# Bilinear sampling weights as clamped ramps on row differences, half of the broadcast ones made on GpSimd

## The chip, the cores and the metric

The kernel runs on one core of a Trainium2 chip. The core has a matrix engine (TensorE, PE in the profile), a vector engine (VectorE, DVE), an engine for pointwise functions (ScalarE, ACT), a general engine (GpSimd, POOL) and a queue engine (SyncE, SP), and 16 DMA engines that serve all queues. The metric is the device time of one execution in microseconds. The kernel before takes 16,853.93 us, the median of three runs from 16,836.08 to 16,859.17.

## The reference

The network has four residual layers on an image batch of 16 x 32 x 128 x 128, in float32. Only layer 1 is touched, and of it the last part. That part samples each image at nine deformed positions per pixel, combines them with a 9-tap convolution and normalises:

```
y      = weight * yk + y_new                     # 9 row positions per pixel
ys     = clip(y_map, 0, H - 1)                   # fractional row
xs     = clip(x_map, 0, W - 1)                   # whole column: c + k - 4
deformed = grid_sample_bilinear(input, (xs, ys)) # two rows, weights 1-|y-p|
out    = conv2d(deformed, dsc_w, dsc_b, stride=(9, 1))
out    = group_norm(out, gn_w, gn_b, 8 groups);   x = x + out
```

The column is always a whole number, so a sample is a mix of two neighbouring rows of one column: row `p` has the weight max(0, 1 - |y - p|).

## The kernel before

The program runs its stages one after the other: layer 0, three stages of layer 1 (offset convolution, scan, sampling), layer 2, and two stages of layer 3. The sampling stage is `layer1_sample`, lines 1031 to 1312.

The interpolation is written as a matrix product over the rows. An image lies in SBUF as `xt`, 128 rows on the partitions, 32 channels times 128 columns along each. For one tap and one image column, the stationary operand is `xt[:, :, xc]` (128 rows x 32 channels) and the moving operand is a 128 x 128 tile that holds, for each of 128 positions `y` (free dimension), the weight of each image row `p` (partition). Four such products stand side by side in the matrix engine (function `sample`, line 1133).

The weights are made as hats. `|y - p|` needs `y` on all partitions. It gets there in two ways: the taps 0 to 3 by a product with a selecting matrix into PSUM (`spread`, matmul in line 1121), read by ScalarE with `Abs` and the bias `nrow` = -p (line 1122) into the tile `ya`; the taps 4 to 7 by a DMA that reads four rows of the position map and writes them to all 128 partitions (`fetch`, line 1111, 1 MB), the tile `yd`, on which ScalarE runs `Abs` in place (`absolutes`, line 1242). VectorE then turns both into min(|y - p|, 1) - 1, the hat with its sign turned (`hats`, line 1126). The ninth tap is made like `ya`, once per four blocks (`eighth`, tile `h8`, `last_tap`). The turned sign is undone in the convolution weights `w4` and `w8` (lines 1103 and 1105).

A block `m` is four image columns; an image has 32 blocks, the 16 images 512. The loop over `m` issues, in this order: on block 12 the loads of the next image (`open_image`, with `xt` in four quarters of eight channels, line 1099); the fetch for block m+3; the products of taps 0 to 3; `Abs` of `yd` and the hat of `ya` for block m+1; the copy of the products out of PSUM (line 1280); the spread for block m+2; the products of taps 4 to 7; the hat of `yd` for block m+1; the second copy (line 1286). Every four blocks follow the convolution (lines 1168 and 1173), a turn to rows on the partitions (line 1185), and the ninth tap. When an image is complete, `finish` normalises it in 22 small steps, one per block, and adds the input `xt` (line 1233); the result is stored by a DMA on GpSimd's queue (line 1234).

`in_order` (line 48) fixes the order of TensorE's, VectorE's and ScalarE's instructions to that of the program. SP, which issues the loads, is ordered by the planner. `yd` has four buffers, so a fetch waits until the products of the block four earlier have read its buffer; `xt` has two, and because `finish` adds the input, a buffer is held until the image after it is about two thirds done.

Of the kernel before, what the change touches and what calls it, by code (L numbers as in the profile page):

```python
# [10 lines left out]
F32 = mybir.dt.float32  # L11
AF = mybir.ActivationFunctionType
ALU = mybir.AluOpType
# [1017 lines left out]
def layer1_sample(tc, w, x1, x2, ymap, sb1, batches=range(B)):  # L1031
# [6 lines left out]


    nc = tc.nc  # L1040
    V, S, M = nc.vector, nc.scalar, nc.tensor.matmul
    W4 = 4 * HW
    NB = HW // 4
    batches = list(batches)
    with ExitStack() as ctx:
# [9 lines left out]
        nrow = load(nc, cp, w["nrow"], "nrow")  # L1055
        avg = cp.tile([P, P], F32, name="avg", tag="avg")
        V.memset(avg, 1.0 / P)

# [28 lines left out]
        def open_image(b):  # L1087
            im = images[b] = {}
            g, j = divmod(b, 4)
            im["Y"] = Y = yp.tile([P, W4], F32, name="Y", tag="Y")  # L1090
            nc.sync.dma_start(Y, ym(b)[0:4].rearrange("k (n f) -> (k n) f", f=W4))
            im["Y8"] = Y8 = yp.tile([P, W4], F32, name="Y8", tag="Y8")
            y8 = ym(b)[8].rearrange("(s q f) -> q s f", q=4, f=W4)
            for q in range(4):
                nc.sync.dma_start(Y8[32 * q : 32 * q + 8], y8[q])
            im["xt"] = xt = xp.tile([P, T, HW], F32, name="xt", tag="xt")
            xg = x1[g][T * j : T * j + T].rearrange("o (r c) -> r o c", c=HW)
            for q in range(4):
                nc.sync.dma_start(xt[:, 8 * q : 8 * q + 8], xg[:, 8 * q : 8 * q + 8])

            s = cb[:, g, j, 0:1]
            im["w4"] = w4 = sp.tile([P, 2, T], F32, name="w4", tag="w4")
            V.tensor_scalar(w4, dw4[:, :, 0:T], s, -1.0, ALU.mult, ALU.mult)
            im["w8"] = w8 = sp.tile([P, P], F32, name="w8", tag="w8")
            V.tensor_scalar(w8, dw8, s, -1.0, ALU.mult, ALU.mult)

        def fetch(m):
            b, n = order[m]
            blocks[m] = bl = {}
            bl["yd"] = yd = hp.tile([P, 4, W4], F32, name="yd", tag="yd", bufs=4)  # L1110
            nc.sync.dma_start(
                yd, ym(b)[4:8, n * W4 : n * W4 + W4].unsqueeze(0).to_broadcast([P, 4, W4])
            )

        def spread(dst, Y, n, k):

            for h in range(2):
                pb = psb.tile([P, 2, W4], F32, name="pb", tag="pb")
                for a in range(2):
                    q = 32 * (2 * h + a)  # L1120
                    M(pb[:, a], sel[q : q + k, n], Y[q : q + k], start=True, stop=True)  # L1121
                S.activation(dst[:, 2 * h : 2 * h + 2], pb, AF.Abs, bias=nrow)  # L1122

        def hats(t):

            V.tensor_scalar(t, t, 1.0, 1.0, ALU.min, ALU.subtract)  # L1126

        def sample(pd, b, todo):

# [5 lines left out]
                    start=True, stop=True, tile_position=(0, 32 * q),  # L1135
                )

        def taps(m, k0, h):
            b, n = order[m]
            pd = psd.tile([P, 4, HW], F32, name="pd", tag="pd")  # L1140
            sample(
                pd, b,
                [
                    (q, i, 4 * n + i + k0 + q - 4, h[:, q, HW * i : HW * i + HW])
                    for i in range(4) for q in range(4)
                ],
            )
            return pd
# [42 lines left out]
        def finish(b):  # L1191

            g, j = divmod(b, 4)
            im = images[b]
            ob, xt = im["ob"], im["xt"]
# [24 lines left out]
            V.tensor_mul(bi, sc, mean.unsqueeze(2).to_broadcast([P, 8, 4]))  # L1220
            V.tensor_sub(bi, rows[:, 1].rearrange("p (a b) -> p a b", b=4), bi)
            yield
            for q in range(4):
                o = slice(8 * q, 8 * q + 8)
                col = [
                    t.rearrange("p a b -> p (a b)")[:, o].unsqueeze(2).to_broadcast([P, 8, HW])
                    for t in (sc, bi)
                ]
                V.tensor_mul(ob[:, o], ob[:, o], col[0])
                yield  # L1230
                V.tensor_add(ob[:, o], ob[:, o], col[1])
# [8 lines left out]
        def absolutes(m):  # L1240
            yd = blocks[m]["yd"]
            S.activation(yd, yd, AF.Abs, bias=nrow)  # L1242

        def near(m):
            b, n = order[m]
# [6 lines left out]
            images[b]["h8", s] = h8  # L1252

        open_image(batches[0])
        NM = len(order)
        for m in range(min(3, NM)):
            fetch(m)
        with in_order(tc, nc.tensor, nc.vector, nc.scalar):
            eighth(batches[0], 0)
            near(0)  # L1260
            absolutes(0)
            near(1)
            hats(images[batches[0]]["h8", 0])
            hats(blocks[0]["ya"])
            hats(blocks[0]["yd"])
            done = iter(())
            for m in range(NM + 6):
                b, n = order[m] if m < NM else (None, m - NM)
                if m < NM:
                    bl = blocks[m]  # L1270
                    bl["ds"] = dp.tile([P, 2, W4], F32, name="ds", tag="ds", bufs=6)
                    if n == 12 and m + NB < NM:
                        open_image(order[m + NB][0])
                    if m + 3 < NM:
                        fetch(m + 3)
                    pd = taps(m, 0, bl["ya"])
                    if m + 1 < NM:
                        absolutes(m + 1)
                        hats(blocks[m + 1]["ya"])
                    V.tensor_copy(bl["ds"][:, 0], pd.rearrange("p i r -> p (i r)"))  # L1280
                    if m + 2 < NM:
                        near(m + 2)
                    pd = taps(m, 4, bl["yd"])
                    if m + 1 < NM:
                        hats(blocks[m + 1]["yd"])
                    V.tensor_copy(bl["ds"][:, 1], pd.rearrange("p i r -> p (i r)"))  # L1286
                s, i = divmod(n, 4)
                if i == 0 and 4 <= m <= NM:
# [6 lines left out]
                elif i == 1 and 5 <= m <= NM + 1:  # L1295
                    turn(bb, ss, oc)
                    if ss == NB // 4 - 1:
                        for _ in done:
                            pass
                        done = finish(bb)  # L1300
                elif i == 2 and m + 2 < NM:
                    nb_, nn = order[m + 2]
                    eighth(nb_, nn // 4)
                elif i == 3 and m < NM:
                    pd = last_tap(b, s, images[b].pop(("h8", s)))
                    ds8 = dp.tile([P, W4], F32, name="ds8", tag="ds8")
                    S.copy(ds8, pd.rearrange("p i r -> p (i r)"))
                    images[b]["ds8"] = ds8
                    if m + 1 < NM:
                        nb_, nn = order[m + 1]  # L1310
                        hats(images[nb_]["h8", nn // 4])
                next(done, None)
            for _ in done:
                pass
# [982 lines left out]
def pack(inp):  # L2297
# [105 lines left out]
    w["nrow"] = -np.arange(P, dtype=f)[:, None]  # L2403

    def conv(a):
        return _diag(a.reshape(a.shape[0], a.shape[1], 9).transpose(1, 2, 0), 4)
# [97 lines left out]
```

## Time and profile before

| | value |
|---|---|
| span of the profiled execution | 16,843.7 us |
| median of the runs | 16,853.93 us |
| PE, DVE, ACT, POOL busy in the whole span | 14,662.1, 14,631.9, 12,582.5, 9,561.6 us |
| sampling stage, 10,855 to 14,030 us: PE, ACT, DVE, POOL busy | 2,890.6, 2,794.6, 2,739.7, 93.2 us |
| granted TensorE clock and DMA share in the stage | 0.90, 0.78 |
| `ya` (L1122), two per block | 1,024 elements, mean 1,251 ns |
| `yd` (L1242), one per block | 2,048 elements, mean 2,421 ns |
| hats of `ya` and `yd` (L1126) | 2,048 elements, mean 1,478 and 1,414 ns |
| ScalarE's wait for the DMA of `yd` in the stage | 47.5 us in 13 waits |

The profiled execution's own time is its span, 16,843.7 us; the runs' median is 10 us longer, as it takes in what lies around the first and last instruction. Busy times overlap between engines. A group's mean duration is that of single instructions, which may overlap at their ends with the next.

### The profile page before, as it was taken

What the parts mean: (1) busy time and instruction counts of PE and PEld (TensorE: products, weight loads), DVE (VectorE), ACT (ScalarE), POOL (GpSimd) and SP (SyncE); (2) the same over time, 40 slices, a digit from 0 to 9 for tenths busy, and PEclk for the clock granted to TensorE, in tenths of its full rate; (3) what the DMA queues carried; (4) which work ended last, traced back from release to release, by engine and by line L of the source; (5) the groups of instructions that cost most, each with busy time, mean ns of one, the idle gap of its engine ahead of it and who ended that gap; (6) DMA issues with size and microseconds to landing.
All of it is one profiled execution on the core that took longest, in us unless ns stands there. A gap on an engine that the chain in (4) does not pass through costs nothing. (4 is left out here: it accounts for less than half of the span.)

```text
span 16843.7 us, 301825 instructions
## 1 busy us (share of the span) xinstructions
PE 14662.1 (87%) x113386; PEld 5677.8 (34%) x113386; DVE 14631.9 (87%) x14520; ACT 12582.5 (75%) x25308; POOL 9561.6 (57%) x17517
## 2 busy tenths in 40 slices
PE   8999999989999888988888888899999997688966
PEld 3333333333333222222222222255555553234421
DVE  9999999999999669999999999888888887788622
ACT  8999999999999557777777677688898883466411
POOL 8999999999999238778887788500000000000012
PEclk9999999999999989899999999899999898788977
DMA  0000000000000854445454445578877789644456
GB/s 22 13 12 13 13 17 13 13 12 13 18 13 8 136 139 164 154 161 163 168 166 163 156 161 168 159 187 197 200 199 194 193 192 195 129 79 83 79 147 201
DMA packets 1553471, 1898.99 MB, mean 113 GB/s; under 512 B 158053, under 2 KB 879710, under 8 KB 1543239
## 3 DMA queue, kind: packets, MB, share of 16 engines
q1 hardware_dynamic: 1440582, 1701.94, 38.7%
q0 software_dynamic: 31552, 127.40, 2.1%
q10 hardware_dynamic: 79872, 50.36, 1.2%
q8 instruction: 892, 14.61, 0.4%
q14 instruction: 573, 4.69, 0.1%
HBM read 1560.92 MB, written 229.64 MB: 106 GB/s over the span
## 5 line engine op out<-in xcount | busy, mean ns | idle before, releaser
L235 POOL TENSOR_SCALAR Rp<-su,nv 128x128 f32<-128x128 f32 x15360 | 5406.1, 371 | 167.7 <-PE pS L241 132.9
L239 ACT ACTIVATE Ra<-su,bv 128x128 f32<-128x128 f32 x15360 | 4625.8, 389 | 405.9 <-PE pS L241 402.6
L224 DVE TENSOR_TENSOR Rd<-pu,nv 128x2048 f32<-128x2048 f32 x2176 | 4856.6, 2275 | 19.6 <-PE pS L241 18.6
L241 PE MATMUL pS<-Rd,zw 128*32 128x512 f32 x17408 | 2794.8, 606 | 380.1 <-DVE Rd L224 379.4
L828 DVE TENSOR_TENSOR_SCAN hh<-dd,state,pd 128x512 f32<-128x512 f32 x2304 | 2823.3, 1267 | 152.6 <-PE py L862 9.6
L849 POOL TENSOR_TENSOR hh<-hh,bc 128x2048 f32<-128x2048 f32 x512 | 2319.0, 4530 | 451.2 <-DVE state L836 437.9
L1234 POOL DMA_DIRECT2D x<-ob x64 | 92.4, 1443 | 3106.4 <-DVE ob L1233 2769.9
L813 PE MATMUL pd<-du,spread 32*128 32x512 f32 x4608 | 1348.8, 659 | 553.3 <-DVE hh L828 545.7
L805 ACT ACTIVATE dd<-dd,m_a 128x512 f32<-128x512 f32 x2304 | 1513.1, 713 | 328.5 <-DMA dd<-dm 322.4
L823 DVE TENSOR_TENSOR pd<-pd,bc 128x1024 f32<-128x1024 f32 x1152 | 1401.0, 1216 | 53.4 <-ACT bc L786 51.4
L241 PE MATMUL pS<-Rp,zw 128*32 128x512 f32 x7680 | 1310.7, 597 | 25.3 <-POOL Rp L235 25.2
L1242 ACT ACTIVATE yd<-yd,nrow 128x2048 f32<-128x2048 f32 x512 | 1239.7, 2421 | 47.6 <-DMA yd<-ymap 47.5
L1122 ACT ACTIVATE ya<-pb,nrow 128x1024 f32<-128x1024 f32 x1024 | 1188.4, 1251 | 86.5 <-PE pb L1121 85.4
L241 PE MATMUL pS<-Ra,zw 128*32 128x512 f32 x7680 | 1235.7, 600 | 0.0
L1121 PE MATMUL pb<-Y,sel 32*128 32x512 f32 (+1 forms) x5120 | 1083.6, 742 | 167.5 <-ACT ya L1122 164.2
L241 PEld LDWEIGHTS pS<-Rd,zw 128*32 128x32 f32 x17408 | 580.8, 109 | 1487.5 <-DVE Rd L224 928.7
L813 PEld LDWEIGHTS pd<-du,spread 32*128 32x128 f32 x4608 | 372.8, 190 | 1594.7 <-DVE hh L828 714.4
L1126 DVE TENSOR_SCALAR yd<-yd 128x2048 f32<-128x2048 f32 x512 | 724.2, 1414 | 191.8 <-ACT yd L1242 190.9
L1126 DVE TENSOR_SCALAR ya<-ya 128x2048 f32<-128x2048 f32 x512 | 756.7, 1478 | 9.2 <-ACT ya L1122 7.6
L1133 PE MATMUL pd<-ya,xt 128*32 128x128 f32 x16384 | 690.7, 311 | 42.7 <-DVE ds L1286 31.3
L1133 PEld LDWEIGHTS pd<-yd,xt 128*32 128x32 f32 x16384 | 539.2, 178 | 469.9 <-issue 231.5
L1839 PE MATMUL ps<-t,W 128*128 128x512 f32 x1280 | 627.8, 637 | 64.2 <-DVE W L1819 56.5
(426 smaller groups left out, 23147.3 us busy)
## 6 DMA issues: line engine op xcount, KB each, us to landing
dd<-dm SPq DMA_DIRECT2D x2304, 256.0 KB
yd<-ymap SPq DMA_DIRECT2D x512, 1024.0 KB
hw<-x SPq DMA_DIRECT2D x192, 512.0 KB
dm<-dt POOLq DMA_DIRECT2D x192, 256.0 KB, 3.6
w<-d SPq DMA_DIRECT2D x512, 73.1 KB
xb<-tok SPq DMA_DIRECT2D x248, 144.0 KB
x<-in_x SPq DMA_DIRECT2D x64, 512.0 KB
x<-o SPq DMA_DIRECT2D x128, 256.0 KB
```

The source lines that it names most:

```text
L224: nc.vector.tensor_tensor(R, st["pu"].unsqueeze(1).to_broadcast([P, 4, 4, HW]), nv[:, :, i::32].rearrange("p t q -> p q t").unsqueeze(3).t ...
L235: nc.gpsimd.tensor_scalar(R[:, q, k], su[:, k], 3.4028234e38, nv[:, k, c], ALU.min, ALU.max)
L239: nc.scalar.activation(R[:, q, k], su[:, k], AF.Relu, bias=bv[:, k, c])
L241: nc.tensor.matmul(st["pS"][32 * q : 32 * q + 32], zw[:, 31 - i : 63 - i], R[:, q], start=first, stop=False, tile_position=(0, 32 * q), sk ...
L805: S.activation(dd[:, r], dd[:, r], AF.Exp, scale=acol[:, dr, d : d + 1])
L813: nc.tensor.matmul(pd[:, a], spread[e, k], st["du"][n][e], start=True, stop=True)
L823: V.tensor_mul(pd, pd, bm.unsqueeze(1).to_broadcast([P, 2, CH]))
L828: V.tensor_tensor_scan(hh[:, r, s], dd[:, r, s], pd[:, a, s], st["state"][:, 4 * i + r : 4 * i + r + 1], ALU.mult, ALU.add,)
L849: G.tensor_mul(hh, hh, st["bc"][1, n].unsqueeze(1).to_broadcast([P, 4, CH]))
L1126: V.tensor_scalar(t, t, 1.0, 1.0, ALU.min, ALU.subtract)
L1133: M(pd[32 * q : 32 * q + 32, i], xt[:, :, xc], h, start=True, stop=True, tile_position=(0, 32 * q),)
L1242: S.activation(yd, yd, AF.Abs, bias=nrow)
```

## The change

The sum over hats is rewritten by parts. With x[p] the rows of the image and y between 0 and 127, the sample is x[0] + sum over p of clamp(y - p, 0, 1) * (x[p+1] - x[p]). The moving operand thus holds ramps, max(y - p, 0) limited to 1, and the stationary operand holds differences of neighbouring rows. The last partition carries row 0: its bias is +1, so that its ramp is always 1.

- The `xt` tile is loaded from rows 1 to 127 and, on its last partition, row 0: two DMAs per quarter in place of one, of 127 rows and of one row.
- The plain rows are loaded as well, in quarters (`quarter`, tile `xq`, two buffers, on SP), and GpSimd subtracts them from `xt` on 127 partitions (`differ`), at the blocks 24 to 27 before the image is used; for the first image before the loop.
- `finish` adds `xq` quarters, loaded again, and no longer reads `xt`.
- `Abs` becomes `Relu` on ScalarE; VectorE's operation becomes a minimum with 1 (`clamps`), still in place.
- The fetch of taps 4 to 7 becomes two fetches of two rows each, `yd` (taps 4 and 5) and `ye` (6 and 7), 512 KB each, both with four buffers. ScalarE and VectorE treat `yd` as before at half the size. GpSimd makes the ramps of `ye` in two operations (`far`): add the bias and maximum with 0, then minimum with 1, two blocks ahead.
- GpSimd's instructions join the fixed order.

```diff
@@ open_image
             for q in range(4):
-                nc.sync.dma_start(xt[:, 8 * q : 8 * q + 8], xg[:, 8 * q : 8 * q + 8])
+                o = slice(8 * q, 8 * q + 8)
+                nc.sync.dma_start(xt[0 : P - 1, o], xg[1:P, o])
+                nc.sync.dma_start(xt[P - 1 : P, o], xg[0:1, o])
-            V.tensor_scalar(w4, dw4[:, :, 0:T], s, -1.0, ALU.mult, ALU.mult)
+            V.tensor_scalar_mul(w4, dw4[:, :, 0:T], s)
...
+        def quarter(b, q):
+            g, j = divmod(b, 4)
+            xq = xp.tile([P, 8, HW], F32, name="xq", tag="xq")
+            xg = x1[g][T * j + 8 * q : T * j + 8 * q + 8].rearrange("o (r c) -> r o c", c=HW)
+            nc.sync.dma_start(xq, xg)
+            return xq
+
+        def differ(b, q):
+            xt = images[b]["xt"][0 : P - 1, 8 * q : 8 * q + 8]
+            G.tensor_sub(xt, xt, quarter(b, q)[0 : P - 1])
@@ fetch
-            bl["yd"] = yd = hp.tile([P, 4, W4], F32, name="yd", tag="yd", bufs=4)
-            nc.sync.dma_start(
-                yd, ym(b)[4:8, n * W4 : n * W4 + W4].unsqueeze(0).to_broadcast([P, 4, W4])
-            )
+            for key, k in (("yd", 4), ("ye", 6)):
+                bl[key] = t = hp.tile([P, 2, W4], F32, name=key, tag=key, bufs=4)
+                nc.sync.dma_start(
+                    t,
+                    ym(b)[k : k + 2, n * W4 : n * W4 + W4].unsqueeze(0).to_broadcast([P, 2, W4]),
+                )
+
+        def far(m):
+            ye = blocks[m]["ye"]
+            G.tensor_scalar(ye, ye, step, 0.0, ALU.add, ALU.max)
+            G.tensor_scalar_min(ye, ye, 1.0)
@@ spread, hats
-                S.activation(dst[:, 2 * h : 2 * h + 2], pb, AF.Abs, bias=nrow)
+                S.activation(dst[:, 2 * h : 2 * h + 2], pb, AF.Relu, bias=step)
-            V.tensor_scalar(t, t, 1.0, 1.0, ALU.min, ALU.subtract)
+            V.tensor_scalar_min(t, t, 1.0)
@@ finish
+                xq = quarter(b, q)
...
-                V.tensor_add(ob[:, o], ob[:, o], xt[:, o])
+                V.tensor_add(ob[:, o], ob[:, o], xq)
@@ loop
-        with in_order(tc, nc.tensor, nc.vector, nc.scalar):
+        with in_order(tc, nc.tensor, nc.vector, nc.scalar, nc.gpsimd):
...
+                    if 24 <= n < 28 and m + NB < NM:
+                        differ(order[m + NB][0], n - 24)
                     if m + 3 < NM:
                         fetch(m + 3)
+                    if m + 2 < NM:
+                        far(m + 2)
...
-                    pd = taps(m, 4, bl["yd"])
+                    pd = taps(m, 4, bl["yd"], bl["ye"])
```

More of the change, by code (lines that the diff above doesn't have):

```diff
@@ L1040, in layer1_sample @@
     nc = tc.nc
-    V, S, M = nc.vector, nc.scalar, nc.tensor.matmul
+    V, G, S, M = nc.vector, nc.gpsimd, nc.scalar, nc.tensor.matmul
     W4 = 4 * HW
@@ L1054, in layer1_sample @@
         ident = load(nc, cp, w["ident"], "ident")
-        nrow = load(nc, cp, w["nrow"], "nrow")
+        step = load(nc, cp, w["step"], "step")
         avg = cp.tile([P, P], F32, name="avg", tag="avg")
@@ L1098, in open_image @@
             for q in range(4):
-                nc.sync.dma_start(xt[:, 8 * q : 8 * q + 8], xg[:, 8 * q : 8 * q + 8])
+                o = slice(8 * q, 8 * q + 8)
+                nc.sync.dma_start(xt[0 : P - 1, o], xg[1:P, o])
+                nc.sync.dma_start(xt[P - 1 : P, o], xg[0:1, o])
             s = cb[:, g, j, 0:1]
             im["w4"] = w4 = sp.tile([P, 2, T], F32, name="w4", tag="w4")
-            V.tensor_scalar(w4, dw4[:, :, 0:T], s, -1.0, ALU.mult, ALU.mult)
+            V.tensor_scalar_mul(w4, dw4[:, :, 0:T], s)
             im["w8"] = w8 = sp.tile([P, P], F32, name="w8", tag="w8")
-            V.tensor_scalar(w8, dw8, s, -1.0, ALU.mult, ALU.mult)
+            V.tensor_scalar_mul(w8, dw8, s)
+        def quarter(b, q):
[7 more added lines that the diff above has]
+            G.tensor_sub(xt, xt, quarter(b, q)[0 : P - 1])
         def fetch(m):
@@ L1121, in spread, with clamps @@
                     M(pb[:, a], sel[q : q + k, n], Y[q : q + k], start=True, stop=True)
-                S.activation(dst[:, 2 * h : 2 * h + 2], pb, AF.Abs, bias=nrow)
-        def hats(t):
-            V.tensor_scalar(t, t, 1.0, 1.0, ALU.min, ALU.subtract)
+                S.activation(dst[:, 2 * h : 2 * h + 2], pb, AF.Relu, bias=step)
+        def clamps(t):
+            V.tensor_scalar_min(t, t, 1.0)
         def sample(pd, b, todo):
@@ L1136, in sample, with taps @@
                 )
-        def taps(m, k0, h):
+        def taps(m, k0, *hs):
             b, n = order[m]
+            w = 4 // len(hs)
             pd = psd.tile([P, 4, HW], F32, name="pd", tag="pd")
@@ L1143, in taps @@
                 [
-                    (q, i, 4 * n + i + k0 + q - 4, h[:, q, HW * i : HW * i + HW])
+                    (q, i, 4 * n + i + k0 + q - 4, hs[q // w][:, q % w, HW * i : HW * i + HW])
                     for i in range(4) for q in range(4)
@@ L1194, in finish @@
             im = images[b]
-            ob, xt = im["ob"], im["xt"]
+            ob = im["ob"]
             st = sp.tile([P, 8, 6], F32, name="st", tag="st")
@@ L1238, in finish, with ramps @@
                 yield
-        def absolutes(m):
+        def ramps(m):
             yd = blocks[m]["yd"]
-            S.activation(yd, yd, AF.Abs, bias=nrow)
+            S.activation(yd, yd, AF.Relu, bias=step)
         def near(m):
@@ L1254, in layer1_sample @@
         open_image(batches[0])
+        for q in range(4):
+            differ(batches[0], q)
         NM = len(order)
@@ L1257, in layer1_sample @@
             fetch(m)
-        with in_order(tc, nc.tensor, nc.vector, nc.scalar):
+        for m in range(min(2, NM)):
+            far(m)
+        with in_order(tc, nc.tensor, nc.vector, nc.scalar, nc.gpsimd):
             eighth(batches[0], 0)
             near(0)
-            absolutes(0)
+            ramps(0)
             near(1)
-            hats(images[batches[0]]["h8", 0])
-            hats(blocks[0]["ya"])
-            hats(blocks[0]["yd"])
+            clamps(images[batches[0]]["h8", 0])
+            clamps(blocks[0]["ya"])
+            clamps(blocks[0]["yd"])
             done = iter(())
@@ L1273, in layer1_sample @@
                         open_image(order[m + NB][0])
+                    if 24 <= n < 28 and m + NB < NM:
+                        differ(order[m + NB][0], n - 24)
                     if m + 3 < NM:
                         fetch(m + 3)
+                    if m + 2 < NM:
+                        far(m + 2)
                     pd = taps(m, 0, bl["ya"])
                     if m + 1 < NM:
-                        absolutes(m + 1)
-                        hats(blocks[m + 1]["ya"])
+                        ramps(m + 1)
+                        clamps(blocks[m + 1]["ya"])
                     V.tensor_copy(bl["ds"][:, 0], pd.rearrange("p i r -> p (i r)"))
@@ L1282, in layer1_sample @@
                         near(m + 2)
-                    pd = taps(m, 4, bl["yd"])
+                    pd = taps(m, 4, bl["yd"], bl["ye"])
                     if m + 1 < NM:
-                        hats(blocks[m + 1]["yd"])
+                        clamps(blocks[m + 1]["yd"])
                     V.tensor_copy(bl["ds"][:, 1], pd.rearrange("p i r -> p (i r)"))
@@ L1310, in layer1_sample @@
                         nb_, nn = order[m + 1]
-                        hats(images[nb_]["h8", nn // 4])
+                        clamps(images[nb_]["h8", nn // 4])
                 next(done, None)
@@ L2402, in pack @@
     w["dsc_rows"] = np.tile(np.stack([i["gn_w"], i["gn_b"]])[None], (P, 1, 1))
-    w["nrow"] = -np.arange(P, dtype=f)[:, None]
+    w["step"] = -np.arange(P, dtype=f)[:, None]
+    w["step"][P - 1] = 1.0
     def conv(a):
```

## The prediction

> **What bounds the kernel now.** I read the busy time by stretches first, to find the stage that changes. Layer 1's sampling runs from about 10,855 to 14,024 us: 3.17 ms of the 16.84. A steady stretch of it (columns: length; busy time of TensorE, weight loads, VectorE, ScalarE and GpSimd with counts; granted clock; DMA share; GB/s):
>
> ```profile
> 11200.00:13000.00 1800.00, 1659.37 (x25842) 974.89 (x25846) 1572.56 (x1677) 1609.15 (x1188) 55.16 (x37) 0.91 0.79 198
> ```
>
> The groups of instructions of that stretch come next; the reader should take from them the block count and ScalarE's two big forms:
>
> ```profile
> L1242 ACT ACTIVATE yd<-yd,nrow 128x2048 f32<-128x2048 f32 x295 | 712.0, 2414 | 27.7 <-DMA yd<-ymap 27.7
> L1122 ACT ACTIVATE ya<-pb,nrow 128x1024 f32<-128x1024 f32 x590 | 688.8, 1257 | 48.2 <-PE pb L1121 48.0
> ```
>
> 295 blocks in 1800 us make 6.10 us a block: TensorE is busy 5.62 us of it, ScalarE 5.45, VectorE 5.33, GpSimd 0.19. Three engines are close to the bound, and the waits say how they are coupled (total us, times, longest):
>
> ```profile
> PEld pb L1121 <- ACT ya L1122: 175.0, 192, 6.1
> ...
> ACT yd L1242 <- DMA yd<-ymap: 27.7, 8, 5.1
> ```
>
> The second line is small, but it is the one that matters here. It falls once per image, and the SP queue in order of time shows where:
>
> ```profile
> 11199.19 8.10 SPq L1099 DMA_DIRECT2D xt<-x  x4
> 11207.39 10.29 SPq L1111 DMA_DIRECT2D yd<-ymap  x4
> ```
>
> The next image's four `xt` loads go out, and the `yd` fetch behind them becomes the end of the chain of waits:
>
> ```profile
> 11207.39 10.69 DMA yd<-ymap
> ```
>
> So a fetch has little slack. One issued undisturbed at 11,194.2 was consumed by ScalarE at 11,210.0, a lead of about 15 us, and most of that a 1 MB fetch at this DMA load needs anyway. A burst of `xt` in front of a fetch already costs 47.5 us over the stage, in 13 waits.
>
> How long does a burst hold a DMA engine? In the stretch from 10,850 to 10,856 us the traffic is nearly all `xt` in 512 B pieces:
>
> ```profile
> DMA packets 3591, 1.81 MB, mean 302 GB/s; under 512 B 47, under 2 KB 3591, under 8 KB 3591
> ```
>
> 3,544 pieces in 6 us on 16 engines are one piece per 27.1 ns and engine. Today's 128-row quarter puts 64 pieces on each engine (1.7 us), a burst of four 6.9 us.
>
> The change loads 127 rows at a time, so the last view is how a copy's rows are dealt to the engines. Each copy leaves 4-byte packets, which I read as one completion mark per engine that it used. In the sampling stretch 6,411 packets are under 512 B; less 37 GpSimd stores at 16, 5,819 remain. 344 copies of 128 rows at 16 marks and 40 copies of 8 rows at 8 marks make 5,824. The scan stage (6,400 to 8,450 us) has copies of 8, 24 and 72 rows:
>
> ```profile
> DMA packets 187262, 331.27 MB, mean 162 GB/s; under 512 B 32577, under 2 KB 33009, under 8 KB 187149
> ...
> dd<-dm SPq DMA_DIRECT2D x1008, 256.0 KB
> dm<-dt POOLq DMA_DIRECT2D x84, 256.0 KB, 3.6
> xb<-tok SPq DMA_DIRECT2D x108, 144.0 KB
> xa<-tok SPq DMA_DIRECT2D x56, 144.0 KB
> xb<-tok SPq DMA_DIRECT2D x108, 48.0 KB
> old<-kept SPq DMA_DIRECT2D x31, 144.0 KB
> kept<-t SPq DMA_DIRECT2D x27, 144.0 KB
> xa<-tok SPq DMA_DIRECT2D x54, 48.0 KB
> ymap<-yo SPq DMA_DIRECT2D x2, 1152.0 KB
> ```
>
> Of 32,577 small packets, 18,432 are the two `ymap` stores (72 x 128 runs of 128 B each) and 1,344 GpSimd's `dm` marks; 12,801 remain. With ten shorter copies from the lines left out, there are 1,008 copies of 8 rows, 228 of 72 and 168 of 24. Marks equal to the largest divisor of the row count up to 16 (8, 12, 12) make 12,816; 16 where there are at least 16 rows would make 14,400, the largest power of two 11,232. The divisor fits to 0.1%. 127 is prime: one engine.
>
> **The change, part by part.** The sum is made against the profiled execution: span 16,843.7 us; the median of the runs, 16,853.9, lies 10 above it.
>
> *`xt` rows 1 to 127.* Each image issues four copies `xt[0:127]` of 127 x 8 pieces. On one engine a copy is 1,016 x 27.1 ns = 27.5 us, four are 110 us, in place of 6.9. `xt`'s other buffer is free as soon as the last taps of the image before have run (before, it waited for VectorE's last add), so nothing makes SP space them. Every `yd` and `ye` fetch behind them has a sixteenth of its rows on that engine and is not complete until they drain. Queued behind: ScalarE stops at its ramps of `yd`, with the `ya` spreads behind it; GpSimd at its first operation on `ye`; VectorE at the `yd` clamp, with the copies that free TensorE's banks behind it. Three blocks of fetched data run out. Once the engine is clear, the next fetches, already issued, land 2.7 us apart, faster than blocks use them, so nothing further is late. Stall: 110 + 2.7 (the fetch's own 32 pieces of 2 KB at 84 ns, their median in the trace's packet records) - 15 of lead = 98 us; less the 3.4 us per image lost today, 94. There are 16 such bursts (the first delays the first taps instead). 16 x 94 = +1,500. Ends: the same 6 us run between 348 and 280 GB/s, so 24 to 29 ns a piece, which gives +1,310 and +1,650; a burst right behind a fetch instead of in front of one leaves 6 us more lead, -100.
>
> *Restart.* After the 3.9 us gap at 11,217 the spreads took 3.08 us and the taps 2.03, against 1.14 and 1.21 at full clock: 3 us a stall, +50. Below 0 it cannot be; +100 at most.
>
> *One-row copies* `xt[127:128]`: 8 pieces, 0.2 us; 64 more issues of about 0.4 us on SP, idle most of the time: 0.
>
> *`xq` loads.* Eight 128-row quarters per image, 8 x 1.7 = 14 us of each engine's 195 us: DMA share 0.79 to 0.86. One at a time they stay inside the lead: 0. If they cost what the burst of four costs today (3.4 us), twice per image: +110.
>
> *`ye`'s ramps on GpSimd.* Two tensor-scalar operations of 1,024. Nearest rows: 371 ns for 128 elements (L235); two-input 2,357 ns for 1,024 and 4,530 for 2,048, which leaves 184 ns fixed. (371 - 184)/128 = 1.46 ns an element, so 1.68 us each, 3.4 a block; floor from the 3,872-wide memset (3.33 us) 0.9 each, ceiling 2.36 each. With `differ` (4 x 2.36 us per image) and the store issue, GpSimd is busy 3.8 us of 6.1. They need `ye` and must end 1.5 blocks before the taps: hidden. In GpSimd's order the store waits for VectorE's add, up to a block, with the next `far` behind it; the slack of about two blocks covers it.
>
> *Taken off.* ScalarE's `yd` goes from 2,414 to about 1,257 ns (the 1,024 form), -1.16 us a block; VectorE's clamp from 1,427 to about 780, -0.65. Matmuls are unchanged, so the floor is TensorE never waiting: 6.10 - 5.62 = -0.48 a block, -245 in 512. Against it stands contention. The nearest row is layer 0, where VectorE's normalisation runs beside GpSimd:
>
> ```profile
> L235 POOL TENSOR_SCALAR Rp<-su,nv 128x128 f32<-128x128 f32 x17 | 6.4, 392 | 0.0
> L175 DVE TENSOR_SCALAR x<-x,cols 128x256 f32<-128x256 f32 x16 | 6.1, 451 | 0.0
> ```
>
> Without the other, they take 366 and 403: +7% and +12%. On 3.2 us of VectorE's SBUF operations a block (clamps 1.47, 0.78 and 0.43, the image's three passes 0.53) that is +0.4, less than the 0.65 saved. The other end: each of the 2.25 clamps a block waits for a whole 1.68 us operation, VectorE reaches 8.5 us, +1,200. I take the row, and of the gain only 0.1 us a block, as all three engines wait on each other in turn: -50.
>
> The Trainium skill speaks against this part (SBUF — State Buffer, Who interferes with whom): a VectorE operation in a two-port mode and any GpSimd operation exclude each other for the whole instruction. Layer 0's pair, both busy all the time, does not show that, but its operands differ from a clamp by a constant. By the rule the two would need 3.2 + 3.7 = 6.9 us a block, +400 in place of -50 and a sum of 18,800.
> On 127 rows the skill (DMA: Bandwidth & Descriptors, Why a DMA increments its semaphore by 16) says outright that such a copy runs on one engine; no copy of this trace has 127.
>
> Sum: 16,844 + 1,500 + 50 - 50 = 18,344, and 10 for the median: 18,350.
>
> **The rivals.**
> - *The rows spread over 16 engines after all* (9%). For: all of today's `xt` loads do. Against: the marks. Then a burst stays near 7 us, no stall is new, and the time is 16,854 - 50 = 16,800, between 16,610 and 17,000. This ends on the other side; it decides from where a burst on the fullest engine stays under the 15 us of lead, that is eight engines or more.
> - *One engine, but the copies interleave with the fetches* (6%). Then that engine's throughput binds: per image 110 + 32 x 2.7 for the fetches + 14 + about 10 for the stores = 220 us against 195. 16 x 25 = +400: 17,250. For: SP's order is planned, and at the start two `xt` copies, a fetch and two more stood in turn. Against: the four stand together in every later image.
> - *GpSimd and VectorE hold each other up, with the rows spread* (5%): +1 us a block, some way to the other end above: 17,350. Against: layer 0's pair.
>
> **How the numbers follow.** The stall has 80%; its own range is 17,800 to 18,950: below, 1,310 - 100 - 245; above, 1,650 + 100 + 110 and 240 of contention. The wanted range reaches down over the two middle cases: 17,250 to 18,950. A measurement here tells 0.2% from no change. Faster by that has 7%, the same 2%, both from the first rival; slower 91%.
>
> **What would show it.** After: per image one gap of 90 to 100 us on all engines, ended by DMA `yd` or `ye`; in it a DMA share near 1/16 and about 19 GB/s; ScalarE's wait for `yd` near 1,500 us in total where it was 47.5. Between gaps, blocks of about 6.0 us with ScalarE at 4.3 and GpSimd at 3.8. Copies landing in a few us would make the prediction wrong, as would gaps ended by GpSimd, or a fetch that does not queue behind the copies.

## The result and the profile after

The changed kernel takes 19,632.64 us (median of four runs, 19,602.26 to 19,667.67) against 16,855.6: a ratio of 1.1639, 95% interval 1.1623 to 1.1656, or +2,777 us. The forecast was 18,350 with a range up to 18,950: right in its direction, 1,280 us too low. The profiled execution has a span of 19,654.7 us, 2,811 more than before, and nearly all of it (2,783) lies in layer 1's sampling stage, which now runs from 10,898 to 16,850 us in place of 10,855 to 14,024. Busy time by stretches, for that stage (columns as in the first row of the prediction):

```profile
10898.00:16850.00 5952.00, 3487.24 (x44862) 2069.79 (x44861) 2665.18 (x2928) 2218.24 (x2065) 4233.94 (x1161) 0.71 0.48 115
```

5,952 us for 512 blocks are 11.6 us a block in place of 6.2. TensorE is busy 59% of it and ScalarE 37%; the busiest engine is GpSimd with 71%, 8.3 us a block, where the prediction had 3.8. The two groups of instructions that it comes from:

```profile
L1132 POOL TENSOR_SCALAR ye<-ye,step 128x1024 f32<-128x1024 f32 x512 | 2283.2, 4459 | 1515.1 <-DMA ye<-ymap 1501.9
L1133 POOL TENSOR_SCALAR ye<-ye 128x1024 f32<-128x1024 f32 x512 | 1712.6, 3345 | 44.6
```

A block of `ye` costs GpSimd 4.46 + 3.35 = 7.8 us, more than a whole block took before. The waits of the stage (10,855 to 16,900 us; total us, times, longest) show two causes side by side:

```profile
ACT yd L1264 <- DMA yd<-ymap: 1994.8, 116, 105.5
...
POOL ye L1132 <- DMA ye<-ymap: 1501.9, 75, 50.0
PEld pd L1153 <- POOL ye L1133: 1176.0, 396, 7.6
```

The first two are waits for fetches, most of them behind the copies of 127 rows: ScalarE's wait for `yd` was 47.5 us before, and with the copies spread (`e1_rows`, below) 557 and 265 us of the two are left. The third is new and was not forecast: 396 times in 512 blocks, TensorE's products of taps 6 and 7 wait for GpSimd, some 3 us each time. The chain that ended last names the same two, the copies' line L1101 on SP and both GpSimd lines (its shares by line, of the whole span):

```profile
DVE hh L828 11%; POOL ye L1132 11%; DVE Rd L224 7%; POOL ye L1133 7%; PE pS L241 6%; SPq L1101 5%; ACT Ra L239 5%; DVE pd L823 5%; PE ps L1869 4%; POOL Rp L235 2%; SPq L1125 2%; DMA ye<-ymap 2%; PE pd L813 1%; SPq L2217 1%; PE ps L544 1%
```

The copies are as slow as forecast, but the burst has another shape. SP's queue in order of time, during one image's loads (start, duration in us):

```profile
11383.50 0.25 SPq L1100 DMA_DIRECT2D xt<-x  x1
11383.81 28.44 SPq L1101 DMA_DIRECT2D xt<-x  x1
11412.30 0.41 SPq L1100 DMA_DIRECT2D xt<-x  x1
11412.82 25.65 SPq L1125 DMA_DIRECT2D yd<-ymap  x1
11438.58 0.40 SPq L1125 DMA_DIRECT2D ye<-ymap  x1
...
11440.17 29.90 SPq L1101 DMA_DIRECT2D xt<-x  x1
11470.18 0.38 SPq L1125 DMA_DIRECT2D yd<-ymap  x1
...
11471.48 29.89 SPq L1101 DMA_DIRECT2D xt<-x  x1
```

L1100 is the copy of 127 rows: its own issue takes 0.3 to 0.4 us. The issue *behind* it, a one-row copy (L1101) or a fetch (L1125), stands for 26 to 30 us, about as long as the copy's 1,016 pieces take (26.1 us at the 25.7 ns below). SP itself is held for that time, so no later fetch can even be issued. And the four copies of the image do not stand together: fetches slip in between. ScalarE's waits for `yd` in this burst, in order of time:

```profile
11444.05 1.15 ACT L1264 ACTIVATE yd<-yd,step 128x1024 f32<-128x1024 f32 x1 [33.71 <-DMA yd<-ymap]
11476.77 1.15 ACT L1264 ACTIVATE yd<-yd,step 128x1024 f32<-128x1024 f32 x1 [28.87 <-DMA yd<-ymap]
11507.58 1.15 ACT L1264 ACTIVATE yd<-yd,step 128x1024 f32<-128x1024 f32 x1 [27.08 <-DMA yd<-ymap]
```

Three waits of 34, 29 and 27 us, 90 us for the image, where one gap of 90 to 100 was forecast. From 11,390 to 11,410 us the DMA view finds one copy running alone:

```profile
DMA packets 780, 0.43 MB, mean 22 GB/s; under 512 B 0, under 2 KB 778, under 8 KB 778
```

778 pieces in 20 us are one per 25.7 ns (27.1 was taken). The DMA share in these 20 us is 0.08, near the 0.06 of one engine in sixteen.

### The profile page after: what moved, and what is told of

Its sections match the earlier page's. It is cut to its first block, busy times and chain, and to the rows that moved or that the text cites. A ratio compares the mean times of both kernels' runs of the same rounds, so it can differ in the third digit from the quotient of the medians.

```text
span 19654.7 us, 304741 instructions
## 1 busy us (share of the span) xinstructions
PE 15295.5 (78%) x113386; PEld 6056.3 (31%) x113386; DVE 14556.9 (74%) x14520; ACT 12003.5 (61%) x25308; POOL 13699.8 (70%) x18605
## 4 chain that ended last, share of the span: by engine, by line
DVE 28%; POOL 21%; PE 20%; SPq 10%; ACT 8%; issue 7%; DMA 5%; DVEq 0%; ACTq 0%; POOLq 0%
DVE hh L828 11%; POOL ye L1132 11%; DVE Rd L224 7%; POOL ye L1133 7%; PE pS L241 6%; SPq L1101 5%; ACT Ra L239 5%; DVE pd L823 5%; PE ps L1869 4%; POOL Rp L235 2%; SPq L1125 2%; DMA ye<-ymap 2%; PE pd L813 1%; SPq L2217 1%; PE ps L544 1%
## 5 line engine op out<-in xcount | busy, mean ns | idle before, releaser
L1132 POOL TENSOR_SCALAR ye<-ye,step 128x1024 f32<-128x1024 f32 x512 | 2283.2, 4459 | 1515.1 <-DMA ye<-ymap 1501.9
L1146 DVE TENSOR_SCALAR yd<-yd 128x1024 f32<-128x1024 f32 x512 | 568.5, 1110 | 1921.3 <-ACT yd L1264 1919.5
L1264 ACT ACTIVATE yd<-yd,step 128x1024 f32<-128x1024 f32 x512 | 615.4, 1202 | 1994.9 <-DMA yd<-ymap 1994.8
L1133 POOL TENSOR_SCALAR ye<-ye 128x1024 f32<-128x1024 f32 x512 | 1712.6, 3345 | 44.6
L1153 PE MATMUL pd<-ye,xt 128*32 128x128 f32 x8192 | 824.4, 362 | 1071.6 <-POOL ye L1133 1070.6
L1142 ACT ACTIVATE ya<-pb,step 128x1024 f32<-128x1024 f32 x1024 | 1187.5, 1219 | 349.9 <-PE pb L1141 337.2
L1153 PE MATMUL pd<-ya,xt 128*32 128x128 f32 x16384 | 762.7, 333 | 556.7 <-DVE ds L1316 442.7
L1316 DVE COPY ds<-pd 128x512 f32<-128x512 f32 x512 | 372.5, 728 | 917.6 <-PE pd L1153 916.6
L1153 PEld LDWEIGHTS pd<-ye,xt 128*32 128x32 f32 x8192 | 625.7, 182 | 1179.6 <-POOL ye L1133 1176.0
```

What stands on the lines that cost most here:

```text
L1132: G.tensor_scalar(ye, ye, step, 0.0, ALU.add, ALU.max)
L1133: G.tensor_scalar_min(ye, ye, 1.0)
L1153: M(pd[32 * q : 32 * q + 32, i], xt[:, :, xc], h, start=True, stop=True, tile_position=(0, 32 * q),)
```

## The experiments

Three theories stood at the start, under the letters that the expectations use. By A, the one-engine copies are the whole loss, and GpSimd only waits. By B, they cost the forecast 1,500, and GpSimd's two ramps the rest, by their own length. By C, GpSimd is nearly all of it. A further rival puts the rest on the other additions (twice as many fetches, with `xq` loads besides). Four kernels, timed together, take the parts apart. Ratios are to the kernel before, with 95% intervals.

**The copies spread, the rest as changed** (`e1_rows`):

```diff
-                nc.sync.dma_start(xt[0 : P - 1, o], xg[1:P, o])
+                nc.sync.dma_start(xt[0:112, o], xg[1:113, o])
+                nc.sync.dma_start(xt[112 : P - 1, o], xg[113:P, o])
```

> The changed kernel with the 127 rows of each xt quarter loaded as 112 and 15 rows, which the divisor rule puts on 16 and 15 DMA engines; GpSimd's part is left as it is. Theory A (the one-engine queue is the whole loss, 2,780 us in 16 stalls of 174 us): 16,700 to 17,000 us. Theory B (two terms that add: stalls of about 1,500 us, and GpSimd as the bound at 7.8 us of ye operations a block): GpSimd's 4,234 us of busy time in the stage become its length, against 3,175 before: 17,900 to 18,100 us. Theory C (GpSimd is nearly all of it, the queue hides behind it): 19,000 us or more.

Measured 18,372.58 us, 1.0904 [1.0886, 1.0922].

**GpSimd's ramps moved to ScalarE and VectorE, the 127-row copies left** (`e2_nopool`):

```diff
             S.activation(yd, yd, AF.Relu, bias=step)
+            S.activation(ye, ye, AF.Relu, bias=step)
...
-                        far(m + 2)
...
+                        clamps(blocks[m + 1]["ye"])
```

> The changed kernel with the ramps of ye made on ScalarE and VectorE beside those of yd, at the same places; the 127-row copies stay. Theory A: about 19,500 us. Theory B: the stalls of the prediction alone, 94 to 106 us each, 16,855 + 1,500 to 1,700 = 18,350 to 18,550 us. Theory C: 16,900 to 17,100 us.

Measured 18,456.54 us, 1.0947 [1.0931, 1.0964].

**Both edits** (`e3_both`):

> Both: rows as 112 and 15, ye on ScalarE and VectorE. What stays of the change is the ramp form, the row differences on GpSimd, the second and third loading of the rows and the split fetch. All theories: no stall and no GpSimd bound, so 16,700 to 16,950 us; over 17,000 would mean a third term (the extra loads, the order fixed on GpSimd).

Measured 16,974.28 us, 1.0068 [1.0053, 1.0083].

**The kernel before, its quarters of the image loaded as 127 rows and one** (`e4_before127`):

```diff
-                nc.sync.dma_start(xt[:, 8 * q : 8 * q + 8], xg[:, 8 * q : 8 * q + 8])
+                o = slice(8 * q, 8 * q + 8)
+                nc.sync.dma_start(xt[0:127, o], xg[0:127, o])
+                nc.sync.dma_start(xt[127:P, o], xg[127:P, o])
```

> The kernel before with one edit: each xt quarter is loaded as rows 0 to 126 and row 127, two DMAs in place of one. Nothing else of the change. If a 127-row copy runs on one engine and fetches queue behind it: 16 stalls of about 94 us, 18,350 us (17,900 to 18,600). Theory A, stalls of 174 us: 19,600 us. If the queue is hidden or the rows are spread: 16,850 to 16,950 us.

Measured 18,366.69 us, 1.0898 [1.088, 1.0917].

This settles the sum. The rest of the change (ramps, double fetches, `xq` loads, `differ`) costs 120 us (`e3_both` less before). The one-engine copies add 1,482 (`e2_nopool` less `e3_both`), and 1,513 when put alone into the kernel before. GpSimd's ramps add 1,398 (`e1_rows` less `e3_both`). Together 3,000, and 2,777 was measured: the two large costs hide 223 of each other. That is in keeping with blocks of 9 us in `e1_rows`: three blocks fetched ahead last longer then, and a late fetch is missed for less time. This reason was not tested by itself. Theories A and C fall. B fits `e2_nopool`, but `e1_rows` is 270 us above what B expected; `e11_differdve` below shows what B lacks. The further rival falls as well: with all the fetches and loads in place, the rows spread and GpSimd relieved, 120 us are left (24 us above the expected range).

ScalarE's wait for `yd` in `e4_before127`, from 10,855 to 15,700 us, shows the stall undisturbed by anything else:

```profile
ACT yd L1244 <- DMA yd<-ymap: 1571.9, 19, 104.3
```

1,571.9 over 16 images is 98 us, the forecast's figure before today's 3.4 was taken off. Here the four copies stand together in 14 of the 16 images, and SP is held for each:

```profile
11391.84 0.26 SPq L1100 DMA_DIRECT2D xt<-x  x1
11392.15 26.67 SPq L1101 DMA_DIRECT2D xt<-x  x1
...
11419.32 25.74 SPq L1101 DMA_DIRECT2D xt<-x  x1
...
11445.57 25.68 SPq L1101 DMA_DIRECT2D xt<-x  x1
...
11471.76 26.00 SPq L1101 DMA_DIRECT2D xt<-x  x1
11497.86 3.22 SPq L1113 DMA_DIRECT2D yd<-ymap  x4
```

From 11,392 to 11,498 SP issues no fetch, and then four at once. The cost is about what it would be if the fetches had been issued and had waited on the slow engine, which is what the prediction assumed. ScalarE's next `yd`:

```profile
11506.10 2.00 ACT L1244 ACTIVATE yd<-yd,nrow 128x2048 f32<-128x2048 f32 x1 [97.50 <-DMA yd<-ymap]
```

It started 8.2 us after the fetch's issue. Without the wait of 97.5 us it would have started at 11,408.6, 16.8 us after the burst began: that is the lead. The three parts make the stall, 106.0 + 8.2 - 16.8, the 97.5 to within rounding. In all 14 such bursts the lead is 15.5 to 17.1 us, and a fetch takes 6.6 to 8.5 us from its issue to its use. In the second image the copies alternate with fetches, and the waits of 15, 25, 24 and 26 us come to 90, little less.

**Other row counts in the kernel before: 124 + 4 and 126 + 2** (`e5_before124`, `e6_before126`; the edit of `e4_before127` with 124 and 126 in place of 127). They test the divisor rule and the terms of the stall: 124 = 4 x 31 should use 4 engines, 126 = 14 x 9 should use 14.

> The kernel before with each xt quarter loaded as 124 and 4 rows. By the divisor rule 124 rows run on 4 engines: 248 pieces x 27.1 ns = 6.7 us, a burst of 27 us, stalls of 27 + 2.7 - 15 - 3.4 = 11 us, 16 of them: 17,030 us (16,950 to 17,150). If only odd or prime counts were hurt, or the rows were dealt out evenly: 16,840 to 16,900 us.

> The kernel before with each xt quarter loaded as 126 and 2 rows. By the divisor rule 126 rows run on 14 engines, 72 pieces each in place of 64, a burst of 7.8 us: 16,850 to 16,900 us, as before within 0.3%. If any copy short of 128 rows fell to one engine: 18,350 us.

Measured 17,159.37 us, 1.0186 [1.0156, 1.0216], and 16,896.36 us, 1.002 [1.0007, 1.0032]: +298, +35, beside +1,513 for 127 rows. The order is that of the rule. With 124 rows an engine gets 248 pieces per copy, 26.9 us for four at 27.1 ns. ScalarE's waits for `yd` (10,855 to 16,000 us):

```profile
ACT yd L1244 <- DMA yd<-ymap: 339.7, 18, 27.4
```

About 21 us for each of 16 bursts, where 11 + 3.4 were expected. One burst, by its first copy, the last issue that a copy holds up, the next fetch and ScalarE's next `yd`:

```profile
11461.20 0.28 SPq L1100 DMA_DIRECT2D xt<-x  x1
...
11483.13 6.38 SPq L1101 DMA_DIRECT2D xt<-x  x1
11489.61 3.41 SPq L1113 DMA_DIRECT2D yd<-ymap  x4
11498.11 2.00 ACT L1244 ACTIVATE yd<-yd,nrow 128x2048 f32<-128x2048 f32 x1 [21.13 <-DMA yd<-ymap]
```

Each copy holds SP for 6.2 to 7.0 us here, and 248 pieces at 25.7 ns are 6.4, which speaks for four engines. In all SP is held for 28.4 us, the fetch takes 8.5 from issue to use, and the lead is 15.8: 28.4 + 8.5 - 15.8 = 21.1. So the lead of 15 was right, and the 2.7 us for the fetch itself was too little by 5 to 6. With one engine that is 6 us in 98; with four it is half of the stall that was expected, and it is why 17,159 came out just above the expected range.

**What makes GpSimd's ramps cost so much.** By `e1_rows` they are 1.4 ms. Either the operations are this slow by themselves, or VectorE's work beside them holds them up. Four kernels, all with the rows spread as in `e1_rows`.

*The clamps given their 1 from a one-column tile* (`e7_oneport`), meant to put VectorE's clamps into a slower form and to see whether GpSimd then runs freely:

```diff
+        one = cp.tile([P, 1], F32, name="one", tag="one")
+        V.memset(one, 1.0)
...
-            V.tensor_scalar_min(t, t, 1.0)
+            V.tensor_scalar_min(t, t, one)
```

> As e1_rows (18,373 us: rows as 112 and 15, GpSimd's two operations on ye kept), but VectorE's clamps take their 1.0 from a one-column tile in place of an immediate number, which layer 0's rows show to be the slower form (403 ns for 256 elements). In e1_rows GpSimd's two operations take 4.54 and 3.44 us on average, 3.70 and 2.77 at the shortest. Theory K1 (the excess of 1.5 us a block is VectorE's clamps in the fast form holding GpSimd up): the two come near 3.8 and 2.9 us and the kernel loses some 600 to 700 us: about 17,700. Theory K2 (GpSimd's own price; VectorE has no part in it): they stay, 18,300 to 18,500 us.

Measured 18,362.62 us, 1.0888 [1.087, 1.0906], the time of `e1_rows`. The groups of instructions from 12,000 to 13,500 us tell why nothing follows:

```profile
L1149 DVE TENSOR_SCALAR ya<-ya,one 128x2048 f32<-128x2048 f32 x164 | 271.9, 1658 | 7.2 <-ACT ya L1145 7.2
```

1,658 ns for 2,048 elements against 1,567 in `e1_rows`: the operand slowed the operation by 6% only, so the lever was not pulled.

*GpSimd does only the first of its two operations, VectorE the minimum* (`e8_half`):

```diff
             G.tensor_scalar(ye, ye, step, 0.0, ALU.add, ALU.max)
-            G.tensor_scalar_min(ye, ye, 1.0)
...
                         clamps(blocks[m + 1]["yd"])
+                        clamps(blocks[m + 1]["ye"])
```

> As e1_rows, but GpSimd makes only the first operation on ye (add and maximum); the minimum with 1 goes to VectorE, right behind its clamp of yd. GpSimd then has 4.5 us of ye and 0.5 of other work a block. Theory B (GpSimd is the bound because the two operations cost more than a block): 16,850 to 17,150 us. If something else of the GpSimd part is the cause (its place in the order, the wait for ye): 18,000 us or more.

Measured 17,438.36 us, 1.0343 [1.0324, 1.0362]: 934 us less than `e1_rows`, but well above the expected range. GpSimd is no longer the bound (1,517 us busy of 2,000), and yet a block takes 7.2 us. Two groups of instructions from 11,300 to 13,300 us, first `e8_half`:

```profile
L1133 POOL TENSOR_SCALAR ye<-ye,step 128x1024 f32<-128x1024 f32 x280 | 1374.7, 4929 | 397.1 <-DMA ye<-ymap 307.6 <-DVE ye L1146 17.5 <-DVE yd L1146 14.4
...
L1146 DVE TENSOR_SCALAR yd<-yd 128x1024 f32<-128x1024 f32 x278 | 373.4, 1343 | 95.9 <-ACT yd L1264 95.8
```

and the same clamp in `e3_both`, where GpSimd has no ramps:

```profile
L1147 DVE TENSOR_SCALAR yd<-yd 128x1024 f32<-128x1024 f32 x316 | 298.8, 946 | 8.2 <-ACT yd L1265 7.2
```

The GpSimd operation lengthens from 3.7 us (the shortest of its kind in the changed kernel) to 4.9, and VectorE's clamp of `yd` from 946 to 1,343 ns. VectorE's busy time per block goes from 1,804.81 / 316 = 5.7 to 1,740.45 / 278 = 6.3 us for the same operations. So both lengthen when they run beside each other. The block of 7.2 us isn't that alone: in the same 2,000 us GpSimd waits 308 us for the fetches of `ye` and ScalarE 247 for those of `yd`.

*No clamps at all on VectorE* (`e10_noclamp`; the limit at 1 of the weights of taps 0 to 5 and 8 is left out):

```diff
         def clamps(t):
-            V.tensor_scalar_min(t, t, 1.0)
+            pass
```

> As e1_rows, with VectorE's clamps of ya, yd and h8 left out altogether (these ramps are then not limited to 1, so part of the computation is missing); GpSimd keeps both operations on ye. e7_oneport left the clamps in the fast form and told nothing. Theory K1 (beside VectorE's clamps GpSimd's two operations grow from 3.70 + 2.77 to 4.54 + 3.44 us): without them they come near 3.8 + 2.9 us, a block from 9.05 to about 7.7 us, 18,373 - 700 = 17,700 us. Theory K2 (they take this long by themselves): durations and time as in e1_rows, 18,300 to 18,450 us.

Measured 17,848.17 us, 1.0596 [1.0576, 1.0615], 524 us less than `e1_rows`. GpSimd's groups from 11,300 to 13,300 us, first with the clamps (`e1_rows`), then without:

```profile
L1133 POOL TENSOR_SCALAR ye<-ye,step 128x1024 f32<-128x1024 f32 x219 | 999.2, 4562 | 131.3 <-DMA ye<-ymap 120.0 <-PE pb L1142 10.0
L1134 POOL TENSOR_SCALAR ye<-ye 128x1024 f32<-128x1024 f32 x220 | 748.3, 3401 | 19.3
```

```profile
L1133 POOL TENSOR_SCALAR ye<-ye,step 128x1024 f32<-128x1024 f32 x249 | 1013.7, 4071 | 148.3 <-DMA ye<-ymap 147.0
L1134 POOL TENSOR_SCALAR ye<-ye 128x1024 f32<-128x1024 f32 x249 | 708.1, 2844 | 21.8
```

7.96 us a block against 6.92: the clamps lengthen GpSimd's pair by 1.05 us, and 512 x 1.05 = 537 accounts for the gain of 524. But 6.9 us remain, above the 6.1 us of a block. The prices of the two operations with the least company are 3.71 and 2.77 us (the minima of the changed kernel; in `e10_noclamp` 3.70 and 2.77), 6.5 us together. What lengthens the pair by the other 0.4 us, without any clamps, was not tested; nearly all of it is in the first operation (4,071 ns).

*The row subtraction moved to VectorE* (`e11_differdve`), since SP in `e1_rows` waits 901 us for it:

```profile
SPq L1114 <- POOL xt L1119: 901.1, 60, 26.2
```

(SP's waits of `e1_rows`, 10,855 to 15,600 us.) L1114 loads `xq`, whose two buffers come free when GpSimd has subtracted; fetches stand behind it in SP's queue.

```diff
-            G.tensor_sub(xt, xt, quarter(b, q)[0 : P - 1])
+            V.tensor_sub(xt, xt, quarter(b, q)[0 : P - 1])
```

> As e1_rows, with the subtraction that makes the row differences on VectorE in place of GpSimd. In e1_rows SP waited 901 us for that subtraction, with the fetches behind it, and a block takes 9.05 us where GpSimd is busy 8.4. If that wait is a cost of its own, GpSimd's 0.33 us a block and most of the 0.6 us of waits go: 17,900 to 18,100 us. If the waits only fill time that GpSimd's bound leaves: 18,150 to 18,250 us.

Measured 18,006.18 us, 1.0688 [1.067, 1.0707], 366 less than `e1_rows` and inside what was expected of a wait with a cost of its own. The stretch from 11,300 to 13,300 us, and GpSimd's two operations in it:

```profile
11300.00:13300.00 2000.00, 1552.02 (x21060) 937.78 (x21064) 1319.82 (x1395) 1053.72 (x968) 1977.58 (x513) 0.80 0.68 161
...
L1133 POOL TENSOR_SCALAR ye<-ye,step 128x1024 f32<-128x1024 f32 x241 | 1107.3, 4595 | 1.4
L1134 POOL TENSOR_SCALAR ye<-ye 128x1024 f32<-128x1024 f32 x241 | 844.1, 3503 | 21.1
```

GpSimd is busy 1,978 of 2,000 us: a pure GpSimd bound, 2,000 / 241 blocks = 8.3 us each. It is the sum of 6.5 for the operations alone, 1.6 by which they are lengthened and 0.2 for the rest. Over `e3_both` (2,000 / 316 = 6.33) that is 1.97 x 512 = 1,009, and 18,006 - 16,974 = 1,032 was measured. The remaining 366 of the 1,398 are the subtraction on GpSimd, and they have two parts. Its own time was 80.1 us in 219.5 blocks, 187 us in 512. And the late `xq` loads held SP with the fetches behind them: GpSimd's idle time goes from 0.68 us a block to 0.09, 300 us in 512, and ScalarE's wait for `yd` in the stage from 557 to 17 us. Against these two stands some 70 us, by which GpSimd's pair lengthens (7.96 to 8.10 us). The block thus goes from 9.1 to 8.3 us, some 415 us in 512, a little more than the 366 measured.

**Can the form pay at all?** Writing the weights with second differences of the rows, x[p+1] - 2 x[p] + x[p-1], makes max(y - p, 0) without any limit at 1, so all clamps go and GpSimd keeps one operation (`v1_second`). With that operation on VectorE, in the clamp's place, GpSimd makes only the differences (`v2_vector`). The rows are spread in both.

```diff
         def differ(b, q):
             xt = images[b]["xt"][0 : P - 1, 8 * q : 8 * q + 8]
-            G.tensor_sub(xt, xt, quarter(b, q)[0 : P - 1])
...
+            nc.sync.dma_start(xm[1:113], xg[0:112])
+            nc.sync.dma_start(xm[113 : P - 1], xg[112 : P - 2])
+            G.tensor_add(xt, xt, xm[0 : P - 1])
+            xq = quarter(b, q)[0 : P - 1]
+            G.tensor_sub(xt, xt, xq)
+            G.tensor_sub(xt, xt, xq)
...
             G.tensor_scalar(ye, ye, step, 0.0, ALU.add, ALU.max)
-            G.tensor_scalar_min(ye, ye, 1.0)
...
-            V.tensor_scalar_min(t, t, 1.0)
+            pass
```

> A version meant to be faster than both: the sum by parts is done twice, so that the weights are plain max(y - p, 0) on second differences of the rows and need no limit at 1. Every clamp goes, GpSimd makes ye in one operation, rows are loaded as 112 and 15. The second differences cost GpSimd three operations per quarter in place of one. GpSimd: 3.8 + 1.0 + 0.2 = 5.0 us a block, ScalarE 4.3, VectorE 2.6, TensorE 5.6: TensorE is the bound, 16,600 to 16,950 us. If GpSimd's fetch of ye comes too late for it, as in e8_half (454 us of waits): about 17,100 us.

> As v1_second (second differences, no clamps; 17,030 us, 6.35 us a block), with the one operation on ye moved from GpSimd to VectorE, to the place where its clamp of yd stood. VectorE has 2.4 us a block in v1_second and goes to about 3.2; GpSimd keeps the differences, about 1.2 us. In v1_second GpSimd waited 262 us in 2,000 for the fetch of ye, which it needs a block earlier than the others need yd, and TensorE waited 182 us for GpSimd. If that early use is what costs: the block comes down by 0.4 to 0.6 us, 16,700 to 16,850 us, faster than the kernel before. If the DMA traffic of the extra loads (share 0.84) is the bound: 17,000 us, unchanged.

Measured 17,030.15 us, 1.0117 [1.0089, 1.0144], and 16,958.62 us, 1.0042 [1.002, 1.0065]. `v2_vector` has VectorE at half load and ScalarE at 71%, and its stretch from 11,300 to 13,300 us reads:

```profile
11300.00:13300.00 2000.00, 1770.64 (x28179) 1046.03 (x28174) 1056.80 (x1435) 1422.35 (x1297) 404.98 (x201) 0.90 0.85 224
```

Still 2,000 / 322 = 6.2 us a block. Its waits in the same stretch say what took the engines' place:

```profile
DVE ye L1142 <- DMA ye<-ymap: 339.3, 60, 13.4
...
ACT yd L1273 <- DMA yd<-ymap: 273.2, 59, 11.7
```

The fetches: `ye` and `yd` come late. Why isn't settled. The extra loads of the image bring the DMA share to 0.85, and the time is near what was expected if that binds (17,000). But SP is also held by loads whose buffers GpSimd frees late, as in `e1_rows`; its waits in the same stretch:

```profile
SPq L1114 <- POOL xt L1128: 172.5, 40, 6.5
SPq L1123 <- POOL xt L1125: 93.0, 31, 5.7
```

No run separates the two. None of these versions is faster than the kernel before.

## Why the prediction was wrong

- **Rows dealt by the largest divisor, 127 on one engine: right.** Read from completion marks alone, it is borne out by one copy at 20 GB/s and by 127, 124 and 126 rows costing +1,513, +298 and +35. The Trainium skill states it for 127 rows (DMA: Bandwidth & Descriptors, Why a DMA increments its semaphore by 16); `e4_before127` agrees.
- **The stall, 16 x 94 = +1,500: right in size** (1,482 and 1,513), in part by luck. The lead of 15 us was right (15.5 to 17.1). The 2.7 us for the fetch itself was not: that is what its pieces take on one engine, while from issue to use it takes 6.6 to 8.5 us in `e4_before127`, and the prediction's own line of before has 10.69 for one. Quicker pieces make up for it (25.7 ns for 27.1, some 6 us in four copies), so that `e4_before127` still shows 98 us an image. And the fetches were taken as "already issued", while SP cannot issue them; in the changed kernel the stall comes in three parts. The rival of interleaved copies (17,250) described that order but priced it as throughput; measured, interleaving saves little (90 us an image in place of 98), because each fetch still waits for the copy in front of it.
- **One-row copies at 0, `xq` loads at 0, restart +50, relief of the engines -50: near enough together.** `e3_both` holds the first two, with the split fetch, and stands at +120. The restart is part of the 1,482 and 1,513 and was not measured alone. The `xq` loads are cheap only while GpSimd is in time: in `e1_rows` they wait for its subtraction with the fetches behind them, some 300 us (`e11_differdve`). The relief can't be read off any run: `v2_vector`, with VectorE at half load, waits for its fetches, and the forecast's floor of "TensorE never waiting" was not reached by any run.
- **`ye`'s ramps on GpSimd, "1.68 us each, 3.4 a block", "hidden": wrong, and the failing step.** They cost 4.46 and 3.35 us, and +1,398 with the rows spread. The 1.46 ns an element came from subtracting the fixed cost of *two-input* operations (184 ns) from a tensor-scalar's 371 ns for 128 elements; the "ceiling 2.36" was also a two-input price. Neither holds: at the shortest, a one-input operation with two steps and a column operand takes 3,710 ns for 1,024 (3.6 ns an element), with one step and a constant 2,767 (2.7). The undivided row, 371 / 128 = 2.9 ns, would have given 3.0 us each, 6.0 a block: still too little, but with the 0.4 of other work no longer hidden in 6.1. Another row of the trace of before shows a one-input operation with two steps at length (two constants, with the elements put in another order). In the groups of the scan stage

```profile
L901 POOL TENSOR_SCALAR yo<-t 72x512 f32<-72x512 f32 x28 | 54.5, 1948 | 0.0
```

1,948 ns for 512 elements are 3.8 ns an element, 3.9 us for 1,024: two of them 7.8 us, more than a block, and "hidden" would have fallen on paper.
- **Contention +7% and +12% from layer 0's pair: too small.** In `e11_differdve` GpSimd's pair is lengthened from 6.5 to 8.1 us, 25%; in `e8_half` VectorE's clamp of `yd` by 42%. But at the forecast's 3.4 us a block even 25% would have stayed hidden on GpSimd; the price came first. The rival "GpSimd and VectorE hold each other up, with the rows spread" had +1 us a block, and the clamps do lengthen GpSimd's pair by 1.05. But its 17,350 left out the price, on top of which this comes: with the rows spread, 18,373 was measured (`e1_rows`).
- **The skill's rule against this part** (SBUF — State Buffer, Who interferes with whom), that one of the two is shut out for the whole instruction, was worth +400 by the prediction's prices. The direction was right. As an exclusive lock it does not show in the durations of `e1_rows`: with GpSimd busy 92% of the time, VectorE's clamp of `ya` takes 1,567 ns against 1,547 without GpSimd's ramps; a lock would make most clamps wait for the rest of a 3 to 4 us operation. Nor would the operations fit one after the other: in the 2,000 us of `e11_differdve`, 241 pairs at 6.5 us and the clamps of `ya`, `yd` and the ninth tap at their lengths in `e3_both` would need some 2,260. In `e1_rows` it is GpSimd that lengthens, by 1.05 us a block.

Of what was said would show it: 19 GB/s (19 to 20) and ScalarE at 4.3 us a block (957.15 / 219 = 4.4 in `e1_rows`) held, and ScalarE's wait for `yd` near 1,500 held roughly (1,995, in parts). One gap per image, "GpSimd at 3.8" and blocks of "about 6.0 us" between gaps did not: three gaps in the image shown, 8.3 us, and 9.1 us with the gaps away (`e1_rows`). One of the signs of being wrong came as well, gaps ended by GpSimd: TensorE's 1,176 us.

## What to carry to other kernels

Before work moves to an engine with idle time, price it from a row of the same engine, the same number of inputs and the same kind of operation, and scale the undivided row; a fixed cost taken from another kind of operation can halve the price, and when the priced work is half a block, that decides whether it is hidden. Cut rows into counts with a large divisor up to 16: 112 + 15 + 1 rows in place of 127 + 1 were worth 1,260 us in the changed kernel and 1,482 without GpSimd's ramps, and a slow copy also holds the queue that issues it. When a kernel has three engines near the bound and DMA at 0.8, look at the fetches before relieving engines by loading more: in `v2_vector` the waits for them took the engines' place.

## What the runs showed of the hardware that was not expected

- A copy on one engine holds its issuing queue: the next issue on SP takes 26 to 30 us, be it a copy of one row or a fetch.
- GpSimd's price per element depends on the form of the operation, not only on its inputs: 2.7 ns for a minimum with a constant, 3.6 ns for add and maximum with a column operand, on the same 128x1024 tile.
- VectorE's minimum with 1 runs at almost the same speed from a one-column tile (1,658 ns for 2,048 elements) as from a constant (1,567).
- Contention between the two is uneven. VectorE's clamps, against `e3_both`: that of `ya` lengthens by 1% in both `e1_rows` and `e8_half`, that of `yd` from 946 ns to 1,132 in `e1_rows` and 1,343 in `e8_half`. GpSimd's first operation takes 4.6 us in `e1_rows` and 4.9 in `e8_half`, against 3.7 at the shortest. What decides between them was not tried.
- The granted TensorE clock is lower where TensorE is busy less. From 11,300 to 13,300 us it is 0.91 at 92% busy before, 0.90 at 90% in `e3_both`, 0.78 at 71% in `e1_rows` and 0.72 at 59% in the changed kernel. With it the products of taps 4 and 5 go from 300 ns (`e3_both`) to 346 (`e1_rows`); as TensorE waits for GpSimd there, this should cost little, but it was not measured.
